# A four-layer network with a selective scan: row direction first, scan inputs made with the tokens

## The chip, the cores and the metric

One core of a Trainium2 chip runs the whole program, in fp32. The metric is the time of one execution on the device, in microseconds. Five engines work side by side, each with a queue of its own that is executed in order: PE (matmul), DVE (vector), ACT (activation functions), POOL (general elementwise work) and SP, which here only issues DMAs. ACT issues some DMAs too.

## What is computed

The input is four images of 64 x 64 tokens with 128 channels. Four layers follow each other for every image: a selective-scan layer, a global attention, a convolutional block, and a neighbourhood attention with its MLP. The change is in the first layer, and in the place of one table of the fourth. The core of the first layer:

```python
xn = _ln(input, ln1_w, ln1_b)
x_, z = jnp.split(xn @ in_proj_w, 2, axis=-1)
xc = _silu(depthwise_conv3x3(x_) + conv_b)             # 256 channels
x0 = xc.reshape(Bn, DI, L)                             # over rows
x1 = jnp.transpose(xc, (0, 1, 3, 2)).reshape(Bn, DI, L)  # over columns
xs = jnp.stack([x0, x1, x0[..., ::-1], x1[..., ::-1]], axis=1)
x_dbl = jnp.einsum('bkdl,kcd->bkcl', xs, x_proj_w)     # 8 + 16 + 16 rows
dts, Bs, Cs = jnp.split(x_dbl, [R, R + N], axis=2)
delta = jax.nn.softplus(jnp.einsum('bkrl,kdr->bkdl', dts, dt_w) + dt_b)
def step(h, t):
    x_t, d_t, B_t, C_t = t
    h = jnp.exp(d_t[..., None] * A) * h + (d_t * x_t)[..., None] * B_t[:, :, None, :]
    return (h, jnp.einsum('bkdn,bkn->bkd', h, C_t))
```

The four directions k = 0 to 3 (rows, columns, rows backwards, columns backwards) are scanned over 4096 tokens with 16 states per channel; their sum is normalized, gated by `silu(z)`, projected back and followed by an MLP. In the fourth layer, attention over 7 x 7 neighbours adds a position bias from the table `rpb`.

## The kernel before

**Inputs of the scan** (`scan_inputs`, L277). For each image, `scan_tokens` (L289) goes over 8 chunks of 512 tokens (8 rows of the image): layer norm, in_proj into a `band` of rows and into the gate, then, one chunk behind (the convolution needs the next chunk's first row), the 3 x 3 convolution as nine diagonal matmuls for each half of the channels, and Silu into `xc`, which stays in SBUF for the whole image. Gate and `xc` also go to DRAM. When all chunks are through, `scan_steps` (L374) makes the inputs of the four directions, columns (`o` = 1, directions 1 and 3) before rows (`o` = 0, directions 0 and 2), two chunks at a time: `px` is x_proj for both directions of the pair, `xdbl` its copy with a one in the bias rows, then for each direction `pd` = dt_proj for both halves of the channels, softplus (Exp and Ln, 1024 columns each) into `delta`, and on POOL `du` = `delta` times `xc` (L418). `bc`, `delta` and `du` are written to DRAM. `px` and `pd` each hold two PSUM banks, and there are two such pairs.

**The scan** (`selective_scan`, L452). For each direction in `ORDER`, each chunk, each half `hf` of the channels and each group `j` of 4 states: SP loads `bc`, and once per half `dt` and `du`, all broadcast over partitions. A unit is one such group for one pair of channel blocks, 512 units an image: POOL makes `dB` (L499), ACT two `dA` = exp (L505), DVE two scans (L507), then the product with C is made by DVE (L512) or, for 5 of 16 units in image 0 and 7 of 16 later, by POOL (L520). Matmuls add the states up into `py` (L553). Directions 0 and 1 are written to `y_first`; direction 3 adds `y_first` of direction 1 and is written to `y_cols`; direction 2 adds `y_first` of direction 0 and the `y_cols` of all chunks, through tiles called `y_before`, and its result is `y`.

**Order of the work.** The program is put in order when it is built: a planner goes through a model of time and gives each engine the ready instruction with the lowest priority number. Work gets numbers in the order of the text; `with priority(...)` moves a part behind. The scan has `SCAN_FIRST`, so it fills what the other work leaves free. `make_bias` (the position bias of layer 3, twelve tables of 1 MB made in one buffer `bt` and stored to DRAM) and `make_layer2` (folded weights) have `SCAN_FIRST // 2`: after the inputs of image 0 and before the scan. Beside the scan of image 0 the inputs of images 1 to 3 are made; beside that of image `img`, the rest of the network for image `img - 1` (`rest`: the layer's output stage, layers 1, 2, 3). The rest of the last image stands alone at the end.

**Memory.** Pools are stacks with a left and a right side; a pool that is opened where an earlier one was closed waits for that one's last readers. The bias and layer 2's preparation are on the right, and `S.psum`, the scan's four PSUM banks, is opened on the right after the inputs of image 0.

Of the kernel before, what the change touches and what calls it, by code (L numbers as in the profile page):

```python
# [50 lines left out]


SCORE_LIMIT, VALUE_LIMIT, STEP_LIMIT = 60.0, 1.0e9, 10.0
ORDER = (1, 3, 0, 2)
BEHIND = 2
ON_POOL = ((1, 4, 7, 10, 13), (0, 2, 4, 6, 9, 11, 13))
SCAN_FIRST = 10_000_000
# [219 lines left out]
def scan_inputs(tc, K, A, D, img):  # L277

    nc = tc.nc
    with ExitStack() as ctx:
        big = ctx.enter_context(tc.tile_pool(name="si", bufs=1))
        xc = big.tile([128, ND, NT], F32, name="xc")
        scan_tokens(tc, K, A, D, img, xc)
        scan_steps(tc, K, A, D, img, xc)


def scan_tokens(tc, K, A, D, img, xc):  # L289
    nc = tc.nc  # L290
    with ExitStack() as ctx:
        pool = ctx.enter_context(tc.tile_pool(name="si_a", bufs=2))
# [3 lines left out]
        ln_w, ln_b = load("ln1_w", [128, 1]), load("ln1_b", [128, 1])  # L296
        in_proj, conv_b = load("in_proj_w", [128, 2 * DI]), load("conv_b", [128, ND])
        diag = load("conv_diag", [128, ND, 9, 128], D.conv_diag)
        together = Together(tc, K)
        bands = {}  # L300
        for c in range(NCH + 1):
            acts = []
            if c < NCH:
# [45 lines left out]
                nc.scalar.dma_start(D.sz[img][c], sz)  # L349
            if c > 0:  # L350
                nc.scalar.dma_start(D.xc[img][c - 1], xc[:, :, span(c - 1)])


def softplus(tc, K, pool, out, x):

    nc = tc.nc
    if not K.general:
        nc.scalar.activation(x, x, AF.Exp)  # L360
        nc.scalar.activation(out, x, AF.Ln, bias=1.0)  # L361
        return
    e, u = (pool.tile(list(out.shape), F32, name=f"softplus_{n}") for n in "eu")
    nc.scalar.activation(e, x, AF.Abs)
    nc.scalar.activation(x, x, AF.Relu)
    nc.scalar.activation(e, e, AF.Exp, scale=-1.0)
    nc.scalar.activation(u, e, AF.Identity, bias=1.0)
    nc.scalar.activation(out, u, AF.Ln)
    nc.vector.scalar_tensor_tensor(e, u, -1.0, e, ALU.add, ALU.subtract)
    nc.vector.tensor_sub(out, out, e)  # L370
    nc.vector.tensor_add(out, out, x)


def scan_steps(tc, K, A, D, img, xc):  # L374


    nc = tc.nc
    with ExitStack() as ctx:
        pool = ctx.enter_context(tc.tile_pool(name="si_b", bufs=1))
        psum = ctx.enter_context(tc.tile_pool(name="si_bp", bufs=2, space=PSUM))  # L380
        load = loader(tc, pool, A, 0)
        x_proj, dt_w = load("x_proj_w", [128, ND, 2, 128]), load("dt_w", [128, 2, DI])
        for o in (1, 0):
            for g in range(NCH // 2):
                xdbl = pool.tile([128, 2, LC], F32, name="xdbl", bufs=3)
                px = psum.tile([128, 2, LC], F32, name="ps2")
                tokens = []
                for i in range(2):
                    c = 2 * g + i
                    if o == 0:  # L390
                        tk = xc[:, :, span(c)].rearrange("p d (a b) -> p d a b", b=H)
                    else:
                        tk = xc.rearrange("p d (h w) -> p d w h", w=W)[:, :, span(c, RC), :]
                    tokens.append(tk)
                    for d in range(ND):
                        nc.tensor.matmul(
                            px[:, i, :].rearrange("p (a b) -> p a b", b=H), x_proj[:, d, o, :], tk[:, d, :, :],
                            start=(d == 0), stop=(d == ND - 1),
                        )
                nc.scalar.activation(xdbl, px, AF.Identity, bias=K.first2)  # L400
                for i in range(2):
                    c = 2 * g + i
                    for b in range(2):
                        k, rows, first = o + 2 * b, slice(64 * b, 64 * b + 1 + R), 64 * b + 1 + R
                        nc.scalar.dma_start(
                            D.bc[img][k][c].rearrange("n w t -> w n t"), xdbl[first : first + 2 * NS, i, :]
                        )
                        pd = psum.tile([128, ND, LC], F32, name="ps2")
                        for d in range(ND):
                            nc.tensor.matmul(  # L410
                                pd[:, d, :], dt_w[rows, o, d * 128 : (d + 1) * 128], xdbl[rows, i, :],
                                start=True, stop=True,
                            )
                        delta = pool.tile([128, ND, LC], F32, name="delta", bufs=3)
                        softplus(tc, K, pool, delta, pd)
                        nc.scalar.dma_start(D.delta[img][k][c], delta)
                        du = pool.tile([128, ND, LC], F32, name="du", bufs=2)
                        nc.gpsimd.tensor_mul(  # L418
                            du.rearrange("p d (a b) -> p d a b", b=H),
                            delta.rearrange("p d (a b) -> p d a b", b=H), tokens[i],  # L420
                        )
                        nc.sync.dma_start(D.du[img][k][c], du)


def make_scan(ctx, tc, K, A):

    nc = tc.nc
    S = SimpleNamespace()
    big = ctx.enter_context(tc.tile_pool(name="ss_big", bufs=1))
    S.pool = ctx.enter_context(tc.tile_pool(name="ss", bufs=2))  # L430
    load = loader(tc, big, A, 0)
    S.A = load("A_log", [128, KD, NJS, NPR, 2])
    nc.scalar.activation(S.A, S.A, AF.Exp)
    nc.vector.tensor_scalar_mul(S.A, S.A, -1.0)
    ds4 = load("Ds", [128, ND, KD])
    total = big.tile([128, ND], F32, name="Dsum")
    nc.vector.tensor_reduce(total, ds4, AX.X, ALU.add)
    S.skip = big.tile([128, ND, 128], F32, name="skip_diag")
    for d in range(ND):
        nc.scalar.activation(S.skip[:, d, :], K.ident, AF.Copy, scale=total[:, d : d + 1])  # L440

    S.pick = big.tile([128, 32], F32, name="pick")
    nc.gpsimd.memset(S.pick, 1.0)
    for base, sign in ((0, 1), (3, -1)):
        nc.gpsimd.affine_select(
            S.pick, S.pick, [[-4 * sign, 32]], ALU.is_ge, 0.0, base=base, channel_multiplier=sign
        )
    S.unit = 0
    return S


def selective_scan(tc, K, S, D, img):  # L452
# [16 lines left out]
    for k in ORDER:  # L469
# [4 lines left out]
        for i in range(NCH):  # L474
            c = NCH - 1 - i if back else i
            for hf in range(2):
# [11 lines left out]
                for j in range(NJS):  # L488
# [39 lines left out]
                    def total(k=k, c=c, hf=hf, j=j, hcs=hcs, made=made, py=py):  # L528
                        if j == 0:
                            py.append(psum.tile([128, LC], F32, name="py"))  # L530
                            before = pool.tile([128, LC], F32, name="y_before", bufs=4)
                            if k == 0:
                                for pp in range(2):
                                    nc.sync.dma_start(
# [5 lines left out]
                                nc.sync.dma_start(before, D.y_first[img][k % 2][c][:, hf, :])  # L540
                                nc.tensor.matmul(py[0], K.ident, before, start=True, stop=False)
                            if k == 2:
                                cols = pool.tile([128, NCH, RC, RC], F32, name="y_before", bufs=4)
                                nc.sync.dma_start(
                                    cols.rearrange("p c a b -> p c (a b)"),
                                    D.y_cols[img][:, :, c, hf].rearrange("c p x -> p c x"),
                                )
                                nc.tensor.matmul(
                                    py[0].rearrange("p (a c b) -> p a c b", a=RC, b=RC), K.ident,
                                    cols.rearrange("p c a b -> p a c b"), start=False, stop=False,  # L550
                                )
# [610 lines left out]
def make_bias(tc, K, A, out):  # L1162
# [4 lines left out]
    NR = 2 * KW - 1  # L1167
    NQ = 9
    with ExitStack() as ctx:
        pool = ctx.enter_context(tc.tile_pool(name="bias", bufs=1, side="right"))  # L1170
        psum = ctx.enter_context(tc.tile_pool(name="bias_p", bufs=4, space=PSUM, side="right"))
        rp = loader(tc, pool, A, 3)("rpbT", [NR, HEADS * NR])

        shifted = pool.tile([NR, 2 * W], F32, name="shifted")
# [441 lines left out]
def everything_again(tc, K, A, D, out):  # L1616
# [3 lines left out]
    for img in range(B):  # L1620
        with ExitStack() as ctx:
            S = make_scan(ctx, tc, K, A)
            S.psum = ctx.enter_context(tc.tile_pool(name="ss_ps", bufs=1, space=PSUM))
            scan_inputs(tc, K, A, D, img)
            selective_scan(tc, K, S, D, img)
        with ExitStack() as ctx:
# [8 lines left out]
def network(tc, A, out):  # L1635
    nc = tc.nc
    with ExitStack() as ctx:
# [26 lines left out]
        with ExitStack() as scan_ctx:  # L1664
            S = make_scan(scan_ctx, tc, K, A)
            make_conv_diagonals(tc, K, A, D.conv_diag)
            with priority(tc, K, SCAN_FIRST // 2):
                make_bias(tc, K, A, D.biasT)
                with tc.tile_pool(name="mk_w2", bufs=1, side="right") as pool:
                    make_layer2(tc, K, A, D, pool)  # L1670
            scan_inputs(tc, K, A, D, 0)
            S.psum = scan_ctx.enter_context(tc.tile_pool(name="ss_ps", bufs=1, space=PSUM, side="right"))
            before = None
            for img in range(B):
                with priority(tc, K, SCAN_FIRST):
                    selective_scan(tc, K, S, D, img)
                if img == 0:
                    for later in range(1, B):
                        scan_inputs(tc, K, A, D, later)
                else:  # L1680
# [88 lines left out]
```

## Time and profile before

| | |
|---|---|
| median of 3 runs | 9151.36 us (9145.9 to 9167.2) |
| the profiled execution | 9166.0 us, its span 9164.3 us |
| PE, DVE, POOL, ACT busy | 80%, 78%, 77%, 62% |
| first and last start of `dB` (L499) | 295.3 and 8155.3 us |
| conv matmuls (L247) in the first 295 us | 122.7 us |
| inputs of images 1 to 3, last `du` | 2158.8 us |
| directions 1, 3, 0, 2 of image 0 begin | 297, 843, 1388, 1946 us |
| scans of images 1, 2, 3 begin | 2475, 4364, 6268 us |

A busy share is that of one engine over the whole span; the engines have their busy stretches at different places. `PE busy` counts pipelined matmuls that overlap. In a line of a timeline or of a window, times are in microseconds from the start of the span; an arrow `<-` after a group names what the engine waited for. `SPq` and `ACTq` lines are issues of DMAs.

### The profile page before, as it was taken

What the parts mean: (1) busy time and instruction counts of PE and PEld (TensorE: products, weight loads), DVE (VectorE), ACT (ScalarE), POOL (GpSimd) and SP (SyncE); (2) the same over time, 40 slices, a digit from 0 to 9 for tenths busy, and PEclk for the clock granted to TensorE, in tenths of its full rate; (3) what the DMA queues carried; (4) which work ended last, traced back from release to release, by engine and by line L of the source; (5) the groups of instructions that cost most, each with busy time, mean ns of one, the idle gap of its engine ahead of it and who ended that gap; (6) DMA issues with size and microseconds to landing.
All of it is one profiled execution on the core that took longest, in us unless ns stands there. A gap on an engine that the chain in (4) does not pass through costs nothing. (4 is left out here: it accounts for less than half of the span.)

```text
span 9164.3 us, 99142 instructions
## 1 busy us (share of the span) xinstructions
PE 7366.3 (80%) x30116; PEld 2795.3 (31%) x30116; DVE 7110.9 (78%) x8483; ACT 5639.9 (62%) x11293; POOL 7049.8 (77%) x3064
## 2 busy tenths in 40 slices
PE   7668686776688887777788987877888878788987
PEld 3222131222322232233322232333222323343333
DVE  1577787778999988988899879988999789863433
ACT  3566665665666666657766656667666666564355
POOL 0888979798899979988899979988999799850000
PEclk8677686877899998788899988888999988889988
DMA  5666767576544555565445555654455555630020
GB/s 163 231 213 230 240 197 266 180 253 236 173 164 174 168 166 191 183 210 181 150 170 176 174 176 181 204 198 163 164 178 172 166 187 187 211 110 4 7 78 29
DMA packets 716653, 1581.72 MB, mean 173 GB/s; under 512 B 203317, under 2 KB 328396, under 8 KB 711757
## 3 DMA queue, kind: packets, MB, share of 16 engines
q1 hardware_dynamic: 585805, 1399.10, 45.2%
q10 hardware_dynamic: 130304, 176.19, 5.4%
q8 instruction: 241, 3.95, 0.2%
q14 instruction: 303, 2.48, 0.1%
HBM read 1280.47 MB, written 283.59 MB: 171 GB/s over the span
## 5 line engine op out<-in xcount | busy, mean ns | idle before, releaser
L499 POOL TENSOR_TENSOR dB<-du,bc 128x1024 f32<-128x1024 f32 x2048 | 4799.9, 2369 | 679.1 <-DMA bc<-bc_dram 217.6
L505 ACT ACTIVATE dA<-dt,w_A_log 128x512 f32<-128x512 f32 x4096 | 2779.3, 689 | 522.8 <-DVE hc L507 283.6
L507 DVE TENSOR_TENSOR_SCAN dA<-dA,state,dB 128x512 f32<-128x512 f32 x2128 | 2626.9, 1272 | 348.9 <-ACT dA L505 179.0
L520 POOL TENSOR_TENSOR hc<-hc,bc 128x1024 f32<-128x1024 f32 x832 | 1966.9, 2368 | 170.2 <-ACT state L516 94.8
L507 DVE TENSOR_TENSOR_SCAN hc<-dA,state,dB 128x512 f32<-128x512 f32 x1456 | 1801.5, 1267 | 320.5 <-PE py L553 112.7
L512 DVE TENSOR_TENSOR hc<-dA,bc 128x512 f32<-128x512 f32 x2432 | 1562.3, 675 | 115.7 <-PE py L553 105.8
L553 PE MATMUL py<-hc,pick 128*32 128x512 f32 x8192 | 1239.9, 688 | 249.0 <-POOL hc L520 195.8
L514 ACT COPY state<-dA 128x1 f32<-128x1 f32 x2128 | 326.2, 157 | 1317.6 <-DVE hc L512 1301.3
L837 PE MATMUL pa<-e,l_v 128*128 128x512 f32 x2048 | 1081.0, 660 | 17.9 <-ACT e L793 17.7
L789 PE MATMUL pair<-l_g,l_f 32*128 32x512 f32 x2048 | 539.8, 678 | 196.7 <-ACT e L793 148.1
L793 ACT ACTIVATE e<-pair 128x1024 f32<-128x1024 f32 (+1 forms) x448 | 508.5, 1135 | 238.1 <-PE pair L789 232.5
L837 PEld LDWEIGHTS pa<-e,l_v 128*128 128x128 f32 x2048 | 381.5, 203 | 687.9 <-issue 638.2
L553 PEld LDWEIGHTS py<-hc,pick 128*32 128x32 f32 x8192 | 215.5, 117 | 1025.3 <-issue 499.4
L1295 PE MATMUL pair<-table,ident 128*128 128x512 f32 x768 | 418.4, 671 | 118.0 <-ACT e L1305 87.6
L410 PE MATMUL ps<-xdbl,w_dt_w 9*128 9x512 f32 x512 | 339.5, 903 | 205.1 <-ACT delta L361 157.4
L247 PE MATMUL ps<-band,w_conv_diag 128*128 128x504 f32 (+3 forms) x1152 | 492.7, 586 | 8.1 <-ACT sz L326 4.1
L507 DVE TENSOR_TENSOR_SCAN dA<-dA,dB 128x512 f32<-128x512 f32 x304 | 357.3, 1213 | 115.9 <-POOL dB L499 86.5
L418 POOL TENSOR_TENSOR du<-delta,xc 128x1024 f32<-128x1024 f32 x128 | 336.1, 2626 | 40.6 <-ACT delta L361 30.0
L219 PE MATMUL ps<-xnT,w_fc_w 128*128 128x512 f32 x512 | 288.7, 697 | 82.4 <-ACT mlp_h L226 32.0
L1305 ACT ACTIVATE e<-pair 128x1024 f32<-128x1024 f32 (+1 forms) x224 | 254.1, 1134 | 136.6 <-PE pair L1299 136.4
L201 PE MATMUL ps<-ident,ln_xn 128*128 128x128 f32 x512 | 128.8, 345 | 257.9 <-ACT ln_xn L198 206.3
L789 PEld LDWEIGHTS pair<-l_g,l_f 32*128 32x128 f32 x2048 | 141.1, 191 | 549.8 <-ACT e L793 277.1
(274 smaller groups left out, 8633.3 us busy)
## 6 DMA issues: line engine op xcount, KB each, us to landing
bc<-bc_dram SPq DMA_DIRECT2D x1024, 512.0 KB
dt<-delta_dram SPq DMA_DIRECT2D x512, 512.0 KB
du<-du_dram SPq DMA_DIRECT2D x512, 512.0 KB
delta_dram<-delta ACTq DMA_DIRECT2D x128, 512.0 KB
du_dram<-du SPq DMA_DIRECT2D x128, 512.0 KB
table<-biasT_dram SPq DMA_DIRECT2D x72, 512.0 KB
y_first_dram<-y_sum ACTq DMA_DIRECT2D x128, 256.0 KB
y_before<-y_first_dram SPq DMA_DIRECT2D x128, 256.0 KB
```

The lines of the kernel that those rows point to most:

```text
L247: mm = nc.tensor.matmul(out[:, r0 - row0 : r1 - row0, c0:c1], lhsT((dy + 1) * 3 + dx + 1), src[:, r0 + dy : r1 + dy, c0 + dx : c1 + dx], s ...
L410: nc.tensor.matmul(pd[:, d, :], dt_w[rows, o, d * 128 : (d + 1) * 128], xdbl[rows, i, :], start=True, stop=True,)
L499: nc.gpsimd.tensor_mul(dB, dus[pp], mid(bct[:, 0, :], 2))
L505: nc.scalar.activation(dA, dts[pp][:, g, :], AF.Exp, scale=S.A[:, k, j, pr, g : g + 1])
L507: nc.vector.tensor_tensor_scan(hg[:, order], dA[:, order], dB[:, g, order], 0.0 if i == 0 else state[:, j, pr, g : g + 1], ALU.mult, ALU.add,)
L512: mm = nc.vector.tensor_mul(hc[:, g, :], dA, bct[:, 1, :])
L520: made.append(nc.gpsimd.tensor_mul(hc, hc, mid(bct[:, 1, :], 2)))
L553: mm = nc.tensor.matmul(py[0][32 * q : 32 * q + 32, :], S.pick, hcs[q // 2][:, q % 2, :], start=(k == 1 and j == 0), stop=(j == NJS - 1),)
L789: nc.tensor.matmul(ps[:, u, :], f[quad, t // 4, span(t % 4, 128)], g[quad, c, :], start=True, stop=True)
L793: made = nc.scalar.activation(e, ps, AF.Exp)
L837: nc.tensor.matmul(pa, v[:, 8 * q + t, :], es[q], start=(t == 0 and q == 0), stop=(t == 7 and q == 3),)
L1295: nc.tensor.matmul(ps[:, u, :], K.ident, t[:, u, :], start=True, stop=False)
```

## The change

`ORDER` becomes (0, 1, 3, 2): rows first. `scan_tokens` and `scan_steps` become one function. `steps(o, c)` makes one chunk's inputs for both directions of a pair, in single PSUM banks from the tokens' own rotation of four, with the two directions' matmuls (rows 0 to 8 and 64 to 72) next to each other and softplus on 512 columns; `steps(0, c - 1)` is called right behind the tokens of a chunk, and `steps(1, c)` for all chunks at the end of the image. `S.psum` is opened in `make_scan`, before all inputs. `make_bias` is called behind the scan of image 0 at the normal priority, thus after the inputs of image 0 and ahead of those of image 1, with its pools on the left. `y_before` has three buffers, not four; `softplus`'s two temporaries, used only in the general path, have one.

```diff
-ORDER = (1, 3, 0, 2)
+ORDER = (0, 1, 3, 2)
...
+        def steps(o, c):
+            if o == 0:
+                tk = xc[:, :, span(c)].rearrange("p d (a b) -> p d a b", b=H)
+            else:
+                tk = xc.rearrange("p d (h w) -> p d w h", w=W)[:, :, span(c, RC), :]
+            px = psum.tile([128, LC], F32, name="ps")
+            for d in range(ND):
+                nc.tensor.matmul(
+                    px.rearrange("p (a b) -> p a b", b=H), x_proj[:, d, o, :], tk[:, d, :, :],
+                    start=(d == 0), stop=(d == ND - 1),
+                )
+            xdbl = pool.tile([128, LC], F32, name="xdbl")
+            nc.scalar.activation(xdbl, px, AF.Identity, bias=K.first2)
+            deltas = [pool.tile([128, ND, LC], F32, name="delta", bufs=2 if K.general else 3) for b in range(2)]
+            for d in range(ND):
+                pds = []
+                for b in range(2):
+                    pd = psum.tile([128, LC], F32, name="ps")
+                    rows = slice(64 * b, 64 * b + 1 + R)
+                    nc.tensor.matmul(
+                        pd, dt_w[rows, o, d * 128 : (d + 1) * 128], xdbl[rows, :], start=True, stop=True
+                    )
+                    pds.append(pd)
+                for b in range(2):
+                    softplus(tc, K, pool, deltas[b][:, d, :], pds[b])
+            for b in range(2):
+                k, first = o + 2 * b, 64 * b + 1 + R
+                nc.scalar.dma_start(D.bc[img][k][c].rearrange("n w t -> w n t"), xdbl[first : first + 2 * NS, :])
+                nc.scalar.dma_start(D.delta[img][k][c], deltas[b])
+                du = pool.tile([128, ND, LC], F32, name="du")
+                nc.gpsimd.tensor_mul(
+                    du.rearrange("p d (a b) -> p d a b", b=H),
+                    deltas[b].rearrange("p d (a b) -> p d a b", b=H), tk,
+                )
+                nc.sync.dma_start(D.du[img][k][c], du)
+
         for c in range(NCH + 1):
...
                 nc.scalar.dma_start(D.xc[img][c - 1], xc[:, :, span(c - 1)])
+                steps(0, c - 1)
+        for c in range(NCH):
+            steps(1, c)
...
-def scan_steps(tc, K, A, D, img, xc):
...
+    S.psum = ctx.enter_context(tc.tile_pool(name="ss_ps", bufs=1, space=PSUM))
...
-                            before = pool.tile([128, LC], F32, name="y_before", bufs=4)
+                            before = pool.tile([128, LC], F32, name="y_before", bufs=3)
...
-        pool = ctx.enter_context(tc.tile_pool(name="bias", bufs=1, side="right"))
-        psum = ctx.enter_context(tc.tile_pool(name="bias_p", bufs=4, space=PSUM, side="right"))
+        pool = ctx.enter_context(tc.tile_pool(name="bias", bufs=1))
+        psum = ctx.enter_context(tc.tile_pool(name="bias_p", bufs=4, space=PSUM))
...
             with priority(tc, K, SCAN_FIRST // 2):
-                make_bias(tc, K, A, D.biasT)
                 with tc.tile_pool(name="mk_w2", bufs=1, side="right") as pool:
                     make_layer2(tc, K, A, D, pool)
             scan_inputs(tc, K, A, D, 0)
-            S.psum = scan_ctx.enter_context(tc.tile_pool(name="ss_ps", bufs=1, space=PSUM, side="right"))
...
                 if img == 0:
+                    make_bias(tc, K, A, D.biasT)
                     for later in range(1, B):
                         scan_inputs(tc, K, A, D, later)
```

More of the change, by code (lines that the diff above doesn't have):

```diff
@@ L282, in scan_inputs @@
     with ExitStack() as ctx:
[L283 to L291, printed above, removed]
         pool = ctx.enter_context(tc.tile_pool(name="si_a", bufs=2))
@@ L298, in scan_tokens @@
         diag = load("conv_diag", [128, ND, 9, 128], D.conv_diag)
+        x_proj, dt_w = load("x_proj_w", [128, ND, 2, 128]), load("dt_w", [128, 2, DI])
+        xc = wpool.tile([128, ND, NT], F32, name="xc")
         together = Together(tc, K)
         bands = {}
+        def steps(o, c):
[33 more added lines that the diff above has]
+                nc.sync.dma_start(D.du[img][k][c], du)
         for c in range(NCH + 1):
@@ L362, in softplus @@
         return
-    e, u = (pool.tile(list(out.shape), F32, name=f"softplus_{n}") for n in "eu")
+    e, u = (pool.tile(list(out.shape), F32, name=f"softplus_{n}", bufs=1) for n in "eu")
     nc.scalar.activation(e, x, AF.Abs)
@@ L371, in softplus @@
     nc.vector.tensor_add(out, out, x)
-def scan_steps(tc, K, A, D, img, xc):
[L377 to L422, printed above, removed]
@@ L542, in total @@
                             if k == 2:
-                                cols = pool.tile([128, NCH, RC, RC], F32, name="y_before", bufs=4)
+                                cols = pool.tile([128, NCH, RC, RC], F32, name="y_before", bufs=3)
                                 nc.sync.dma_start(
@@ L1622, in everything_again @@
             S = make_scan(ctx, tc, K, A)
-            S.psum = ctx.enter_context(tc.tile_pool(name="ss_ps", bufs=1, space=PSUM))
             scan_inputs(tc, K, A, D, img)
```

## The prediction

> **What bounds the kernel now.** I read the busy shares by slice first, then the instructions of the scan (how many, how long), then the windows between the turning points, and last the waits of the start. The page's group table, columns: busy us, mean ns, idle before.
>
> ```profile
> L499 POOL TENSOR_TENSOR dB<-du,bc 128x1024 f32<-128x1024 f32 x2048 | 4799.9, 2369 | 679.1 <-DMA bc<-bc_dram 217.6
> L520 POOL TENSOR_TENSOR hc<-hc,bc 128x1024 f32<-128x1024 f32 x832 | 1966.9, 2368 | 170.2 <-ACT state L516 94.8
> ```
>
> The `dB` product is made once per unit of the scan, 512 units an image, so counting it in a window is counting the scan's progress. Its first start is 295.3 and its last 8155.3; the 1,000 us after that are layers 1 to 3 of the last image and have no scan to hide behind. So the span is three stretches: start (295), scan with the rest of the network beside it (7,870), tail (1,000). Counts of `dB` in windows that end where a stage of the other work ends (columns: window, POOL busy on this line, count, clock, DMA share, GB/s):
>
> ```profile
> 555.00:790.00 235.00, 128.46 (x56) 0.92 0.53 179
> 790.00:1090.00 300.00, 166.30 (x72) 0.60 0.78 267
> 1090.00:1330.00 240.00, 137.56 (x59) 0.92 0.58 186
> 1330.00:1620.00 290.00, 152.67 (x65) 0.63 0.72 256
> 1620.00:1885.00 265.00, 145.25 (x62) 0.89 0.54 183
> 1885.00:2160.00 275.00, 148.70 (x64) 0.65 0.79 274
> 2160.00:2478.00 318.00, 187.33 (x80) 0.80 0.57 190
> 2478.00:4392.00 1914.00, 1212.16 (x518) 0.88 0.53 179
> ```
>
> The first six rows are tokens and steps of images 1, 2, 3 in turn: 378 units in 1605 us, 0.235 per us, whichever of the two runs. Then 0.25 with only the output stage of image 0 beside it, and 0.27 over image 1. The two kinds of window are slow for different reasons (columns: PE, PEld, DVE, ACT, POOL busy and counts, then clock, DMA share, GB/s):
>
> ```profile
> 555.00:790.00 235.00, 201.19 (x612) 80.17 (x616) 179.35 (x243) 163.26 (x389) 167.10 (x73) 0.92 0.53 179
> 790.00:1090.00 300.00, 190.52 (x473) 53.27 (x465) 233.02 (x258) 180.64 (x330) 295.84 (x126) 0.60 0.78 267
> ```
>
> Tokens: PE 86% with POOL at 71%. Steps: POOL 99% (32 `du` products of 2.64 us beside the scan), PE 64% at a low clock. What follows each image hangs on its scan: the last `y` of image 0 leaves at 2479.8 and layer 1 begins at 2536.5; for image 3 it is 8182.7 and 8318. The output stage takes up its chunks as direction 2 writes them, so a scan that ends sooner moves all behind it.
>
> The start, on SP's queue (start, duration) and on the engines:
>
> ```profile
> 122.47 2.16 SPq L1226 DMA_DIRECT2D bt<-T  x3
> 124.67 1.43 SPq L305 DMA_DIRECT2D x<-in_x  x1
> 126.14 0.60 SPq L1226 DMA_DIRECT2D bt<-T  x1
> 130.15 0.33 SPq L1227 DMA_DIRECT2D biasT_dram<-bt  x1
> ...
> POOL w_diag L889 <- DMA biasT_dram<-bt: 208.3, 1, 208.3
> ...
> 272.10 5.66 POOL L418 TENSOR_TENSOR du<-delta,xc 128x1024 f32<-128x1024 f32 x2 [17.76 <-ACT delta L361]
> 295.25 6.95 POOL L499 TENSOR_TENSOR dB<-du,bc 128x1024 f32<-128x1024 f32 x3 [2.17 <-DMA du<-du_dram]
> ```
>
> The loads of `x` stand in one queue between the twelve rounds of the bias (13 to 14 us each, one `bt` buffer), so the tokens take till 246 us, though the conv matmuls are 122.7 us and the in_proj matmuls 47.6; layer 2's preparation waits 208 us for the bias to leave its memory, and `x_proj_w` is issued only at 255.9.
>
> **What the Trainium skill says.** ScalarE: Activation LUTs, What ACT_TABLE_LOAD costs: an ACTIVATE costs some 280 ns fixed plus 0.833 ns a column. The trace agrees roughly: 1010 ns for 1024 columns, 594 to 694 for 512, so halving a tile adds 0.2 to 0.35 us. TensorEngine Tiling, Key Properties: tiles in different rows run in parallel. The trace agrees for 32-row tiles (L789: 2048 matmuls of 678 ns in 539.8 us busy); for the two 64-row groups it shows little. DMA, Issuing engines are not separate DMA queues: all share the same 16 DMA engines, so the moved bias traffic still meets the scan's loads; the trace has share 0.78 in the steps windows.
>
> **The change part by part.**
>
> *Start.* Direction 0 needs only chunk 0 of the tokens. In this trace the first conv matmul is at 36.6. Eighteen of them (36 took 14.9) end at 44, Silu with its table load and the load back (1.28 + 1.4 + 1.28) at 48. From the first x_proj matmul (259.0) to the first `dB` (295.25) the old start took 36 us; for one chunk instead of two I take 4 off, so 48 + 32 = 80, and 85 with some slack for layer 2's 20.8 us `pow` on POOL, now early. Bounds: 75 and 120. Gain of the start: 210 us.
>
> *What goes under the scan in exchange.* The tokens of image 0, its steps and the bias. Tokens with direction 0's steps till about 300 (215 us from 85), direction 1's steps till 435 (16 tiles at the old 8.4 us, 32 of them having taken some 270). The scan goes on meanwhile; it uses a chunk in about 68 us (16 units at 0.235) and one is made in about 33, so it isn't starved.
>
> *Interleaved steps.* Per chunk of the tokens two `du` (5.3 us) go to POOL, which has 29% free there; ACT gets 4 x 2 activations of 0.6 and `xdbl` 0.7, 5.5 us; PE some 4 us. All three fit better than the old separate stage, but ACT rises to some 80%. Old: 535 us an image (1605/3). If the tokens swallow direction 0's steps whole, 29 us a chunk becomes 34: 270 + 135 = 405. If nothing is gained, 535. I take 470. The four-bank rotation shared by tokens and steps is why I don't take 405: a `pd` bank is held over Exp and Ln on a busy ACT, and PE behind it is in order. Splitting adds 64 halves x 2 x 0.2 = 13 us to ACT per image, inside the 470. Row groups save at most half of the L410 time (384 matmuls, 252 us in three images) on a PE that isn't the bound of the steps: 0.
>
> *Bias.* Twelve rounds as before, beside the scan: 160 us without traffic, 205 taken (bounds 160 to 280); 26 us of DVE. It stands ahead of image 1's inputs, in the same memory. On SP a `biasT` store waits some 6 us for its `bt` loads and the scan's `bc`, `dt`, `du` loads queue behind; four `bc` buffers are 8 units, 30 us ahead, and cover it. Without cover: 24 waits x 6 = 144 us. The scan runs at 0.27 meanwhile.
>
> *Sum for image 0,* with 0.23 per us beside inputs (a little under 0.235 for the denser ACT): 85 to 435, 80 units; to 640, 55; three inputs of 470 to 2050, 324; together 459. The other 53 at 0.25 take 212: the scan ends at 2262 against 2480, 218 sooner. The bounds: 405 and 0.24 end it at 2220, 535 and 0.22 at 2320.
>
> *Behind it.* Image 0's output stage starts at 2050, 210 us ahead of the scan's end, not 310: 10 to 20 lost. Order (0,1,3,2) puts direction 2 straight behind 3, whose `y_cols` it reads; halves alternate, so what it reads is a half chunk (26 us) old when asked for: 0, bounds 0 and 10 per image. `y_before` with 3 buffers: direction 2 takes two per half, and SP waits there already; image 2's direction 2, columns total, times, longest:
>
> ```profile
> SPq L540 <- PE py L541: 90.1, 11, 15.0
> ```
>
> 8 us at a time under the same 30 us cover. Three buffers shift which tile waits, not on which half: 10 us for all, bounds 0 and 200. `S.psum` allocated early and `xc` moved between pools: nothing. Gain 218 - 15 - 10 = 193. Against the profiled execution, 9164.3 span and 9166.0 in all: 8973. The median of the runs is 15 less than that execution: 8958, stated as **8955**.
>
> **Rivals.**
> 1. *The inputs become the late ones* (0.15). No denser packing, and the bias in front: inputs end at 640 + 1605 = 2245, the output stage begins only then, layer 1 at 2560, not 2537. The scan is 200 us ahead and no longer the bound; images then follow at the pace of the other work: layers 1 to 3 of image 0 took 1530 (2537 to 4067), the output stage after them 439 while it waited for the scan, without that wait perhaps 350, so 1880 an image; the last layer 1 begins at 2560 + 3 x 1880 = 8200, against 8318: gain 118, 9035. For it: ACT and four banks. Against: POOL's free third in the tokens windows.
> 2. *SP starves the scan in direction 2, slower* (0.06). A half chunk has two `y_before` loads, with three buffers the second waits for the tile of the half in progress and `bc` behind it. There are 64 such halves; above 3 us lost in each the gain of 193 is gone, at 6 us the time is 8955 + 384 = 9340. Against: the cover of 30 us.
> 3. *The scan doesn't start early* (0.06): scheduling leaves the first `dB` near 250, because POOL, SP or the banks are held by foreground work. Gain 0 to 60: 9120. Against: nothing before it is left but chunk 0.
>
> **How the numbers follow.** The forecast has 0.73, its own range 8865 to 9030 (bounds of inputs' length, rate and bias). To leave out no more than 2 in 10 the range must take in most of rival 1: 8865 to 9075. A measurement here can't tell less than about 0.2% (18 us) from none. Faster: 0.73 + 0.15 + most of rival 3, less what the unpriced new schedule may spoil, 0.90; same 0.03; slower 0.07.
>
> **What would show it.** First `dB` at 75 to 120 and not at 295; last `du` of the inputs at 1950 to 2150; last `y` of image 0 near 2260; images 1 to 3 at 1863 to 1914 us each as before; tail 1,000. Wrong if inputs end after 2250, if direction 2 takes more than the present 470 to 530 us, or if SP's waits on L541's successor grow beyond 90 us in a direction.

## The result and the profile after

The changed kernel takes 9039.01 us (median of 4, 9031.73 to 9044.53) where the kernel before, run beside it, takes 9158.97: ratio 0.987, 95% interval 0.9853 to 0.9887. In a later set it took 9031.68 against 9156.85, ratio 0.9858 (0.9842 to 0.9875). It is faster by some 120 us (1.3%), inside the range, at 0.6 of the gain forecast. Its profiled execution took 9043.9 us with a span of 9042.2.

The start did what the forecast said, a little later. SP's queue, POOL and ACT in the changed kernel (start, duration, then the work):

```profile
20.82 20.82 POOL L867 TENSOR_TENSOR w_last<-w_last,mhalf 128x128 f32<-128x128 f32 x1
42.69 0.34 SPq L901 DMA_DIRECT2D w_cv_dram<-w_cv  x1
45.44 0.33 SPq L166 DMA_DIRECT2D w_ln_w<-in_L_conv_ln_w  x1
48.20 0.78 ACT L202 ACTIVATE xnT<-ps,w_ln_b,w_ln_w 128x512 f32<-128x512 f32 x1 [14.19 <-DMA w_ln_w<-in_L_conv_ln_w]
90.16 4.66 POOL L328 TENSOR_TENSOR du<-delta,xc 128x1024 f32<-128x1024 f32 x2 [47.00 <-ACT delta L397]
120.49 11.55 POOL L485 TENSOR_TENSOR dB<-du,bc 128x1024 f32<-128x1024 f32 x5 [25.68 <-DMA du<-du_dram]
```

The tokens' weights are queued on SP behind stores of layer 2's preparation, which wait for the 20.8 us `pow`; so the first conv matmul is at 65.6, not 36.6, and the first `dB` at 120.5, not 85.

The count of `dB` in the changed kernel, windows cut where its stages end: image 0's tokens with the rows' steps, its columns' steps, the bias, inputs of images 1, 2 and 3, then the scan of image 1 (columns: window, POOL busy on the line, count, clock, DMA share, GB/s):

```profile
65.00:365.00 300.00, 144.25 (x62) 0.87 0.61 215
365.00:525.00 160.00, 81.60 (x36) 0.61 0.74 259
525.00:770.00 245.00, 150.59 (x65) 0.53 0.78 247
795.00:1245.00 450.00, 248.99 (x107) 0.77 0.67 239
1250.00:1735.00 485.00, 278.30 (x119) 0.79 0.71 244
1750.00:2210.00 460.00, 265.53 (x113) 0.82 0.71 252
...
2228.00:4115.00 1887.00, 1193.07 (x509) 0.88 0.53 181
```

From the first in_proj matmul of image 1 (779) to the end of the last `du` of image 3 (2213) the inputs take 1434 us, 478 an image; cut in the same way it was 1595 before, 532 an image. The scan goes on at 0.24 per us beside them; the scan of image 0 ends at 2226, 248 us sooner than before. But the inputs end 51 us later than before. The windows of all engines show what the new stage looks like, for image 2 (PE, PEld, DVE, ACT, POOL busy and counts):

```profile
1250.00:1735.00 485.00, 360.99 (x1084) 123.81 (x1076) 390.51 (x462) 332.44 (x757) 441.87 (x188) 0.79 0.71 244
```

POOL is at 91% and PE at 74% over this window, in place of a stage with PE at 86% and POOL at 71% and another with POOL at 99%. The Trainium skill (Perfetto Trace Analysis, Optimization Strategy) suggests interleaving where the most contended engine changes from one regime to the next; here an image's inputs fell by 54 us (532 to 478), and a run below gives some 35 of them to the interleaving.

What becomes of the 248 us is read from two instructions. Layer 1 of an image begins with the matmuls on `w_Wq`, its output stage with the first load of `y`. The kernel before, then the changed one (timelines of PE and of SP, start and duration):

```profile
2536.49 1.92 PE L757 MATMUL pair<-xT,w_Wq 128*32 128x512 f32 x16 [0.22 <-ACT dA L505]
8318.15 1.92 PE L757 MATMUL pair<-xT,w_Wq 128*32 128x512 f32 x16 [0.83 <-DVE x L1584]
...
2168.68 0.43 SPq L604 DMA_DIRECT2D y<-y_dram  x1
7951.03 0.43 SPq L604 DMA_DIRECT2D y<-y_dram  x1
```

```profile
2518.83 3.17 PE L743 MATMUL pair<-xT,w_Wq 128*32 128x512 f32 x16 [2.47 <-DMA w_Wk<-in_L_conv_Wk]
8199.24 1.92 PE L743 MATMUL pair<-xT,w_Wq 128*32 128x512 f32 x16 [0.84 <-DVE x L1570]
...
2224.79 0.43 SPq L590 DMA_DIRECT2D y<-y_dram  x1
7898.41 0.43 SPq L590 DMA_DIRECT2D y<-y_dram  x1
```

With the images between, all from the same two instructions:

| stage | before, us | after, us | sum of the difference |
|---|---|---|---|
| start to output stage of image 0 | 2169 | 2225 | +56 |
| output stage, image 0 | 368 | 294 | -18 |
| layers 1 to 3, image 0 | 1530 | 1501 | -47 |
| output stage, image 1 | 439 | 424 | -62 |
| layers 1 to 3, image 1 | 1513 | 1511 | -65 |
| output stage, image 2 | 417 | 431 | -51 |
| layers 1 to 3, image 2 | 1515 | 1513 | -53 |
| output stage, image 3 | 367 | 301 | -119 |
| layers 1 to 3, image 3 | 846 | 843 | -122 |

The output stages of images 1 and 2 kept about their length, though the scan of image 1 now ends 329 us before that image's layer 1, not 142, and that of image 2 362, not 169. Some of image 1's loads of `y` had waited for the scan's writes before (16.7 us in all), yet its stage took 439 us then and 424 now: it also holds the MLP of layer 3 for the image before. So the end of the scan had not set the length of these stages before either.

What shrank are the first and the last output stage, by 74 and 66 us, for two different reasons. SP's waits ahead of the loads of `y` in the kernel before, image 0 and then image 3 (columns: total, times, longest):

```profile
SPq L604 <- DMA y_dram<-y_sum: 24.0, 3, 10.8
SPq L604 <- PE pv L626: 39.4, 6, 14.9
```

Image 0's loads waited for the scan's writes: each of the last five was issued 2 to 3 us behind one (the last at 2481.8, its write at 2479.8). Image 3's loads, as far as the profile shows, did not; they waited for matmuls of the stage itself. What left the last stage is work of the scan that had stood in it (window of the last output stage before and after; columns PE, PEld, DVE, ACT, POOL busy and counts, then clock, DMA share, GB/s):

```profile
7951.00:8318.00 367.00, 286.44 (x1096) 153.21 (x1096) 199.88 (x349) 229.83 (x490) 157.74 (x68) 0.85 0.34 112
7898.00:8199.00 301.00, 234.70 (x872) 133.53 (x872) 49.11 (x195) 160.84 (x337) 0.00 (x0) 0.88 0.17 53
```

PE is busy 78% of both windows, and of the 224 matmuls that are gone 200 are the scan's (L553 before, L539 after). That this shared work is the reason for the 66 us fits these counts; it was not isolated. The 29 us by which layers 1 to 3 of image 0 got shorter are not explained.

The other work, one stage behind the other, is a chain of its own, and after the change it is the late one. The last `dB` starts 268 us sooner (8155.3 to 7887.0), but the program ends only 122 us sooner: what follows the last `dB` grew from 1,009 to 1,155 us.

### The profile page after: what moved, and what is told of

Its sections match the earlier page's. It is cut to its first block, busy times and chain, and to the rows that moved or that the text cites. A ratio compares the mean times of both kernels' runs of the same rounds, so it can differ in the third digit from the quotient of the medians.

```text
span 9042.2 us, 99354 instructions
## 1 busy us (share of the span) xinstructions
PE 7228.6 (80%) x30116; PEld 2738.4 (30%) x30116; DVE 7119.0 (79%) x8483; ACT 5646.5 (62%) x11581; POOL 7048.5 (78%) x3064
## 5 line engine op out<-in xcount | busy, mean ns | idle before, releaser
L539 PE MATMUL py<-hc,pick 128*32 128x512 f32 x8192 | 1256.6, 693 | 388.0 <-POOL hc L506 273.3
L539 PEld LDWEIGHTS py<-hc,pick 128*32 128x32 f32 x8192 | 213.4, 117 | 1152.9 <-issue 472.7
L247 PEld LDWEIGHTS ps<-band,w_conv_diag 128*128 128x128 f32 x1152 | 221.6, 193 | 282.1 <-issue 263.1
```

Source lines behind the costliest of these rows:

```text
L247: mm = nc.tensor.matmul(out[:, r0 - row0 : r1 - row0, c0:c1], lhsT((dy + 1) * 3 + dx + 1), src[:, r0 + dy : r1 + dy, c0 + dx : c1 + dx], s ...
L539: mm = nc.tensor.matmul(py[0][32 * q : 32 * q + 32, :], S.pick, hcs[q // 2][:, q % 2, :], start=(k == 1 and j == 0), stop=(j == NJS - 1),)
```

## The experiments

I call this reading theory L (late is the other work) and set it against theory S: the scan is still the bound, and its gain is lost later in the scans. A rival from the prediction (SP starving the scan in direction 2) is tried by itself. All runs start from the changed kernel.

**Bias with four buffers.**

```diff
-                bt = pool.tile([128, HEADS, RC, W], F32, name="bt")
+                bt = pool.tile([128, HEADS, RC, W], F32, name="bt", bufs=4)
```

> The changed kernel with four bt buffers for the position bias instead of one, nothing else; the same twelve tables are made. Theory L (the other work is late: inputs of images 1 to 3 end at 2210, the scan of image 0 is done at 2228 and has been overtaken as the bound): the bias stage shrinks from 238 us to some 100, inputs end near 2080, layer 1 of image 0 begins near 2400 instead of 2519, and the time falls by 80 to 140 us, to 8900 to 8960. Theory S (the scan is still the bound and the missing gain is lost in the scan of images 1 to 3): the bias is off the path, the time stays within 20 us of 9039.

9022.09 us, ratio 0.9856 (0.984 to 0.9873): far from L's forecast, inside S's span, and not told apart from the changed kernel. The stage did shrink (memsets from 527.2 to 664.5, not from 528.9 to 751.2), but the inputs end only 52 us sooner of the 76 that the last store gained, and layer 1 of the last image 26. L's number missed, and by the time alone the run speaks for S. But the stages of the other work do begin sooner, so it does not decide between the theories.

**Columns first again.**

```diff
-ORDER = (0, 1, 3, 2)
+ORDER = (1, 3, 0, 2)
```

> The changed kernel with ORDER = (1, 3, 0, 2) as before, so that the scan begins only when all tokens and the first columns' inputs of image 0 are made; nothing else. Theory L: the scan of image 0 begins near 350 and ends near 2440, 210 us later, but layer 1 of image 0 still waits for the inputs and begins near 2500 to 2530; the scan then is just in time and the whole is 0 to 60 us slower than the changed kernel, 9040 to 9100. Theory S (the early start of the scan passes through to the end): 200 to 230 us slower than the changed kernel, about 9250.

9105.69 us, ratio 0.9946 (0.993 to 0.9963): 67 us slower than the changed kernel, slightly above L's span and far from S's 9250. The first `dB` is at 341.3, 221 us later, and the scan of image 0 ends 179 us later (image 1 begins at 2405, not 2226). Yet layer 1 of image 0 begins at 2507.2, 12 us sooner; the loss comes at the other end, where the last output stage takes 350 us (7911 to 8260.9), not 301. Its loads of `y` wait for no write of the scan there either, the last one comes 56 us after the last write; but 160 of the scan's matmuls stand in it, not 8. So most of what rows first gives the scan doesn't reach the end.

**Steps apart from the tokens.**

```diff
-                steps(0, c - 1)
-        for c in range(NCH):
-            steps(1, c)
+        for o in range(2):
+            for c in range(NCH):
+                steps(o, c)
```

> The changed kernel with the rows' steps of an image called after all its tokens, ahead of the columns' steps, instead of behind each chunk; nothing else. The scan of image 0 begins later, near 330. If interleaving is what shortened the inputs of an image from 535 to 470 us, they go back to 520 to 540, image 0's inputs take some 60 us more too, and under theory L the time rises by 150 to 250 us, to 9190 to 9290. If single banks and row groups are what shortened them, the inputs stay at 470 to 490 an image and the time rises by the late start alone, 0 to 80 us.

9234.4 us, ratio 1.009 (1.0074 to 1.0107): slower than the kernel before. The three inputs take 1540 us (802 to 2342), 513 an image. So of the 54 us that an image's inputs lost, some 35 are the interleaving and some 18 the rest of the rewriting. They end 130 us later than in the changed kernel, layer 1 of image 0 begins 135 us later (2653.8), that of image 3 178 later (8377.5), and the time is 195 us longer, inside the span that was given for the interleaving. But the 195 us are not the interleaving's alone: the first `dB` is at 280.3, so 160 us of the early start are taken back with it; columns first, which takes back 221 us of it and leaves the interleaving, costs 67.

**Layer 2's preparation behind the first inputs.**

```diff
-            with priority(tc, K, SCAN_FIRST // 2):
-                with tc.tile_pool(name="mk_w2", bufs=1, side="right") as pool:
-                    make_layer2(tc, K, A, D, pool)
             scan_inputs(tc, K, A, D, 0)
+            with tc.tile_pool(name="mk_w2", bufs=1, side="right") as pool:
+                make_layer2(tc, K, A, D, pool)
```

> The changed kernel with the preparation of layer 2 (folded weights) called behind the inputs of image 0 and ahead of the scan, at the normal priority, instead of ahead of both; nothing else. In the changed kernel SP holds the tokens' weights behind three stores that wait for the 20.8 us pow on POOL, until 45 us. Theory L: the tokens start some 25 us sooner, first dB near 95 instead of 120, and all the other work moves up by 20 to 30 us: 9010 to 9020. Theory S: the scan starts 25 us sooner too and gains the same, so this run does not tell them apart; it prices the wait at the start. If the preparation now delays the steps or the scan, 0 or a loss of some 20 us.

9035.47 us, ratio 0.9874 (0.9857 to 0.989): no difference, where L expected 9010 to 9020. The first `dB` does come at 97.1 instead of 120.5, so the wait at the start is priced at 23 us of the scan; but the bias begins only 17 us sooner and the inputs end at 2208.6, 4 sooner. That a scan which starts sooner takes a share of the engines from the other work would fit this; it was not traced.

**One table of the bias made, stored twelve times.**

```diff
-                bt = pool.tile([128, HEADS, RC, W], F32, name="bt")
-                nc.vector.memset(bt, FAR)
-                for tile_, q0, q1, at in group:
+                if c == 0 and i == 0:
+                    bt = pool.tile([128, HEADS, RC, W], F32, name="bt")
+                    nc.vector.memset(bt, FAR)
+                for tile_, q0, q1, at in group if c == 0 and i == 0 else ():
```

> The changed kernel with only the first of the position bias's twelve tables made; the other eleven stores write the same buffer, so eleven tables are copies (that part of the computation is left out; each of the twelve stores stays). The bias stage falls from 238 us to 50 to 90. Theory L (the chain of the other work is the bound, the scan of image 0 has some 230 us to spare): inputs end 110 to 150 us sooner, layer 1 of image 0 begins near 2380 and the end comes 70 to 150 us sooner, 8890 to 8970; the first kernel run with four buffers, whose stage took 137 us, gained 17 in all, so a result near 9010 would mean that what is saved there is given back in the inputs and in later stages, by the scan that then stands against them. Theory S: within 20 us of 9039.

8974.62 us, ratio 0.9805 (0.9788 to 0.9821), below both intervals of the changed kernel: 64 us less than its first measurement and 57 less than its second, just outside the weak end of L's span (8970) and well outside S's 20 us. This is the run that decides between the two. Nothing of the scan was touched, and its end hardly moves (last `dB` 7908.1, in the changed kernel 7887.0), yet the time falls. Nor is it the work left out: the bias stage keeps DVE busy for 19 us less and PE as before (69 us, 68 in the changed kernel). What went besides are 32 of the 36 loads into the buffer and the waits for them. The same two instructions in this kernel:

```profile
2422.30 1.92 PE L743 MATMUL pair<-xT,w_Wq 128*32 128x512 f32 x16 [0.92 <-ACT xT L638]
8125.32 1.92 PE L743 MATMUL pair<-xT,w_Wq 128*32 128x512 f32 x16 [0.83 <-DVE x L1571]
...
2094.25 0.43 SPq L590 DMA_DIRECT2D y<-y_dram  x1
3908.13 0.43 SPq L590 DMA_DIRECT2D y<-y_dram  x1
5839.80 0.43 SPq L590 DMA_DIRECT2D y<-y_dram  x1
7788.78 0.43 SPq L590 DMA_DIRECT2D y<-y_dram  x1
```

Against the changed kernel the output stages begin 131, 112, 114 and 110 us sooner: the lead is carried through four images nearly whole. The last of them takes 337 us, not 301, and so 74 arrive at layer 1 of image 3. Its loads of `y` wait for no write of the scan; but the scan now ends 119 us after this stage begins (its last `dB`), and 128 of its matmuls stand in the stage, not 8.

**Two `y_before` buffers.**

```diff
-                            before = pool.tile([128, LC], F32, name="y_before", bufs=3)
+                            before = pool.tile([128, LC], F32, name="y_before", bufs=2)
```

(and the same for `cols`)

> The changed kernel with two y_before buffers instead of three; nothing else. It doubles the cut that the change made. Rival 2 of the prediction (SP held by y_before starves the scan in direction 2) with the scan as the bound: each of the 64 halves of direction 2 loses 3 us or more, 200 us or more in all. Theory L with a real hold: direction 2 takes longer (500 us become 520 or more), but the end moves by 0 to 40 us, since the scan has 200 us to spare from image 0 on. If the three buffers cost nothing: direction 2 unchanged at 465 to 530 us and the time within 20 us of 9039.

9053.9 us, ratio 0.9893 (0.9877 to 0.991): 15 us above the first measurement of the changed kernel, with overlapping intervals, and 22 above the second, whose interval ends just below; at most a small loss, far from the 200 us of rival 2. Image 2's direction 2 takes 449 us (5532 to 5981), in the changed kernel 475. SP's wait for such a buffer in it, with three buffers and with two (columns: total, times, longest):

```profile
SPq L530 <- PE py L527: 105.2, 12, 16.1
```

```profile
SPq L526 <- PE py L527: 108.0, 14, 12.5
```

In the kernel before, with four, it was 90.1 in 11 waits. The queue does stand there, and direction 2 is not longer for it.

**No row groups.**

```diff
-            for d in range(ND):
-                pds = []
-                for b in range(2):
+            for b in range(2):
+                pds = []
+                rows = slice(64 * b, 64 * b + 1 + R)
+                for d in range(ND):
...
-                for b in range(2):
-                    softplus(tc, K, pool, deltas[b][:, d, :], pds[b])
+                for d in range(ND):
+                    softplus(tc, K, pool, deltas[b][:, d, :], pds[d])
```

> The changed kernel with each direction's two dt_proj matmuls and softplus together, direction after direction, so that neighbouring matmuls use the same rows; nothing else. If the row groups matter, the 128 pairs of an image lose some 0.4 us each on PE, 10 to 25 us an image in the inputs, and 40 to 80 us in all. If PE isn't what the steps wait for (as the prediction held): within 20 us of 9039.

9018.64 us, ratio 0.9848 (0.9831 to 0.9864): if anything faster, but the repeat of the changed kernel has 0.9858, so no difference. The groups of the dt_proj matmuls (columns: busy, mean ns, idle before), with row groups and without:

```profile
L317 PE MATMUL ps<-xdbl,w_dt_w 9*128 9x512 f32 x512 | 176.8, 769 | 121.2 <-ACT xdbl L310 68.0 <-ACT delta L397 51.8 <-ACT state L500 1.4
```

```profile
L317 PE MATMUL ps<-xdbl,w_dt_w 9*128 9x512 f32 x512 | 225.8, 785 | 86.1 <-ACT xdbl L310 60.5 <-ACT delta L397 24.7 <-ACT state L500 0.8
```

The durations add up to 394 us in 176.8 us busy with row groups, and to 402 us in 225.8 without: the records overlap in both, more with row groups. That fits the Trainium skill (TensorEngine Tiling, Key Properties), where different tiles can execute in parallel, and PE is busy 49 us less. But the idle time ahead of these matmuls grows by 35 us and the kernel is no faster, so PE's time on them is not what the steps wait for. (An image has 64 such pairs, not the 128 of the expectation.)

**Loads of x by ACT.**

```diff
-                nc.sync.dma_start(xt, token_tiles(A["x"][img], c))
+                nc.scalar.dma_start(xt, token_tiles(A["x"][img], c))
```

> The changed kernel with the tokens' loads of x issued by ACT instead of SP; nothing else. In the changed kernel the third x load stands on SP behind the du stores and its layer norm waits 48 us, and the tokens of image 0 take 300 us where the conv matmuls need 123. Theory L: image 0's tokens end 30 to 80 us sooner, and the time falls by 15 to 60 us, 8980 to 9025. If the tokens of image 0 are held by ACT and PE instead, no change within 20 us.

A miss for both: 9076.27 us, ratio 0.9921 (0.9902 to 0.994), 37 us slower. SP's queue was not what held the loads: ACT issues three of them at 59.2, 98.5 and 139.9 us, where SP had issued them at 60.6, 101.7 and 141.9, and the layer norms of image 0 wait 76 us for `x` instead of 84. Image 0 gains 6 us (its bias begins at 523.3, not 528.9), the inputs end 14 us later, and the output stages begin 18 to 36 us later. Why moving 32 issues costs that was not pursued.

**Three edits together** (four bias buffers, layer 2's preparation later, no row groups).

> The changed kernel with three edits of the runs before together: four bt buffers, layer 2's preparation behind the inputs of image 0, and the two dt_proj matmuls direction after direction. Theory L (what shortens the chain of the other work ahead of image 0's output stage arrives at the end, until the scan's end takes over): the three gains of 17, 4 and 20 us add up to 30 to 70 us, 8970 to 9010. If the gains of the single runs were only another draw of the planner's order: within 25 us of 9039, 9015 to 9065.

9019.87 us, ratio 0.9854 (0.9837 to 0.987): outside L's span and inside that of another draw. The inputs end 51 us sooner (2161.8), the first output stage begins 55 sooner and layer 1 of the last image 21. Two to three fifths of such a lead reach the last layer 1: 21 of 55 us here, 26 of 53 with four buffers, 74 of 131 with one table. Where the other work was shortened L had the direction right, and its forecasts of the gain were too large each time.

**The changed kernel again.**

> The changed kernel again, unaltered, on the same chip and in the same rounds as the run with the three edits: 9030 to 9050, as measured first. It is the base for the small differences.

9031.68 us in the same set as the three edits: 12 us apart, inside the intervals. No edit of the real work was shown to beat the changed kernel.

## Why the prediction came out as it did

*The start.* 35 us late (120.5, at the upper bound), mostly for a reason that it named and took too lightly: `pow` on POOL, though through SP's queue and not through POOL's own. It hardly mattered: with layer 2's preparation moved, 23 us of it came back and the time stayed the same.

*Inputs.* An image's inputs were nearly right (470 forecast, 478 measured), and the interleaving is their main cause (35 of the 54 us gained). The rate was 0.24, better than the 0.23 taken, and the scan of image 0 ended at 2226, not at 2262.

*The term that was mis-sized* is what stands in front of those three. "Direction 1's steps till 435" was 525, and the bias of "205 taken" lasted from there to the next inputs' first in_proj matmul at 779, some 250. With 24 us more in the three inputs that makes 2213 and not 2050. In image 0 the tokens with the rows' steps lasted till 365 us, not 300, and the columns' steps took 160 us, not 135. With the scan beside them these inputs took 472 us from their first in_proj matmul, as long as those of a later image.

*The step that failed* is "so a scan that ends sooner moves all behind it", and with it the sign "tail 1,000". The scan's end did come sooner, by 248 us in image 0 and by 268 at the last `dB`; but the tail grew from 1,009 to 1,155 us, and of a gain priced at 193 us some 120 arrived. The step was read from the distances between the last `y` and layer 1 for images 0 and 3, 57 and 135 us, and from loads of `y` that follow the writes. The second distance is more than twice the first, as those of images 1 and 2 are (136 and 165), which already spoke against one common wait. And only image 0's stage was really longer for waiting on the scan: image 3's loads waited for no write, and the stages of images 1 and 2 take as long now (424 and 431 us, against 439 and 417) though the scan ends some 190 us sooner before layer 1. Columns first shows it from one side (a scan 179 us later costs 67), the single bias table from the other (other work 131 us sooner, the scan's end no sooner: 57 to 77 gained).

*Rival 1* had the mechanism: the inputs became the late chain. That its numbers fit stage for stage (inputs at 2245, measured 2213; layer 1 at 2560, 2519; the last layer 1 at 8200, 8199; 9035, 9039) is in part luck. It assumed no denser packing, 535 us an image, where there were 478, and the bias done at 640, where it was 779; the two errors nearly cancel. Its pace of 1880 us an image took an output stage of 350 us; the stages of images 1 and 2 took 424 and 431 and that of image 3 301, and the mean came to 1893. I held it at 0.15 because I judged it by the packing of the inputs, which went well, and not by the sum of all that was put ahead of them. The measured time lies in the range because the range took this rival in, not because the forecast's sum held.

*Rivals 2 and 3* did not happen. SP's wait for a `y_before` buffer did grow beyond the 90 us named as a sign, to 105.2, but image 2's direction 2 took 475 us with three buffers and 449 with two. Bias on SP: the scan ran at 65 units in 245 us, 0.265, as priced (0.27).

Open is how the engines divide between the two chains, and where the leads go. With four buffers the bias's last store came 76 us sooner, the next inputs' first in_proj matmul 53 and the inputs' end 52; with one table 169, 140 and 126. Most of this loss thus comes before the inputs start; it wasn't traced to an engine. Returning the bias to the start under the new order was not tried, since the scan's PSUM banks and the tokens' fill all eight.

## What to carry to other kernels

Where two chains of work share a core, list both chains' turning points for every round before pricing a gain on one of them: a gain that shows in the first and the last round only is worth just those two. A load that stands right behind a write doesn't prove that its stage waits: image 1's stage had such waits and was only 15 us longer. A stage that moves out of an idle start into the middle isn't hidden if it stands in the chain that is late; price it with all that follows in the same memory. And two stages with different full engines gain from being woven together: taken back, with part of the early start, it costs 195 us here, and the order alone 67.

## What was not expected of the hardware

A `pow` over 128 x 128 elements kept POOL for 20.82 us; a product over eight times as many took 2.37. With neighbours in two row groups the same 512 matmuls kept PE busy for 22% less (176.8 us, not 225.8), and the kernel was not faster for it.
